# Two ends of a graph-and-attention layer: where the row work of two batches stands in the queues

## The chip, the cores and the metric

The kernel runs on one core of one Trainium2 chip. The time is the device time of one execution in microseconds, and a kernel's time is the median of its runs. The core has a matrix engine (TensorE, PE in the profile; PEld is its weight load), a vector engine (VectorE, DVE), an activation engine (ScalarE, ACT), a general engine (GpSimd, POOL) and a sync engine (SyncE, SP) whose queue issues every transfer of this kernel. Each engine takes its own instructions in the order in which they were written and waits on semaphores for those of others.

## The reference, cut to what matters

All numbers are float32. There are 16 batches of 1024 rows by 256 columns, and one 1024 by 1024 adjacency matrix. Two layers follow one another, each with a residual and a layer norm:

```python
# layer 0
agg = einsum('nm,bmd->bnd', A_hat, features)          # A_hat: the adjacency, normalised
h   = relu(_batchnorm(agg @ W1.T + b1, g1, be1))
out = _batchnorm(h @ W2.T + b2, g2, be2)              # statistics over all 16 batches
x   = _layernorm(x + out)
# layer 1, for each batch
c_adj = mean(x, axis=-1)                              # one mean per row
A     = abs(abs(sigmoid(c_adj[m] - c_adj[n]) - 0.5) - 0.5) * 2
Wg    = adj * (A + A.T) / 2                           # the gated adjacency
q     = relu((x.T @ Wg) * para)                       # the queries, by channel
k, v  = split(x @ kv_w)
out   = softmax(q k^T * scale) v                      # 4 heads of 64
x     = _layernorm(x + out)
```

The second batch norm of layer 0 needs its statistics over all batches, so layer 1 can't begin before layer 0 has ended.

## The kernel before

Layer 0 runs first and leaves its result, still without the second batch norm, in HBM (`yT`, as 128 by 128 blocks); the first batch's is fetched into SBUF before layer 0 ends. Layer 1 is the function `fast`. It goes batch by batch through 16 attention steps of each batch: two halves of 512 queries (`hf`), two pairs of heads (`pair`), four pairs of 128 keys (`cp`). A step writes scores to PSUM (`scores`, L783), takes exponentials on ScalarE (`exps`, L795), adds them up on VectorE for the denominators (`sums`, L801 and L804) and multiplies them with the values (`attend`, L819). TensorE is given the scores of step k+1 before the weighted sum of step k. After the last step of a pair the result is copied to SBUF (L830, L831) and, for all but the last half of the last batch, written to HBM.

Around the steps stands the work for the batches before and after. For the batch that comes two later: its rows are fetched (`load`: `yT` at L443, the residual at L447), scaled and shifted by the batch norm on GpSimd (`bn2_q`, L610), transposed and added on VectorE (`rows`, L614 and L615), given their statistics (`ln1_a`, with GpSimd's small operations at L66, L68 and L632) and normed on ScalarE (`ln1_b`, L642, which also sums each row). For the next batch: transposed rows (`x1_t` on TensorE, L671, for the first two batches), row means and the row of all means (`means` L675 and L677, `crow` L688 for batch 0; for the others one transpose at L692, a copy at L694, and a round trip through HBM at L695 and L696 that spreads it over the partitions), the gates (`wg_a` on ScalarE, L706 to L709; `wg_b` on VectorE, L715 and L716, after which the next block of the adjacency is loaded into the freed tile, L417), keys and values (L732, L743), and the products with the gated adjacency that give the queries (`graph`, L757; `queries`, L765 and L766). For the batch that has ended: the denominators (`dens`, L846 and L848), their reciprocals (`recips`, L857 and L859), and for each pair of row blocks `fetch_o` (L872), `finish_a` (transpose, division, residual and statistics: L888 to L901) and `finish_b` (norm on ScalarE, L909, and store, L912). In the last half of the last batch the result doesn't go through HBM: `finish_a` transposes it on TensorE (L885).

The order is written out by the program itself. `put(w, t, f, ...)` notes a piece for slot t of batch w; a slot is two steps, and a batch has eight. The last loop takes two slots at a time: `arrange` orders their pieces (those for TensorE spread among the long ones), all of them are issued, and then four attention steps. Pieces thus stand only ahead of every fourth step. `range_so_far` and `range_all` check that the denominators lie in a safe range; the flag of `range_all` is read at the end.

Batch 0 has nothing before it, so its row work, the keys, the values and the first three gates are issued outright ahead of the loop, with GpSimd's and ScalarE's work for it alone. Its queries come from `graph0` (L1074), which holds all four products in PSUM and goes through the eight row blocks one by one; they run in the slots of batch -1, one block in each (`opening`), with the remaining gates. Batch 1's row work stands in the same slots, by `put(b - 2, ...)`: `load` of row pair j in slot j, and what follows in the slots after it. `load` uses two buffers for the rows of `yT` and two for the residual; the adjacency has four.

Of the kernel before, what the change touches and what calls it, by code (L numbers as in the profile page):

```python
# [9 lines left out]
F32 = mybir.dt.float32  # L10
# [12 lines left out]
def gnn_norm_attention_kernel(  # L23
# [543 lines left out]
    def fast():  # L567
      with ExitStack() as fx:
# [48 lines left out]
        def begin(b):  # L617
            x1Ts[b] = x1Tp.tile([P, CT, N], F32, tag="x1T", name=f"x1T_{b}")
            css[b] = sm.tile([P, NT], F32, tag="cs", bufs=2, name=f"cs_{b}")
# [188 lines left out]
        def by_pe(b, hf):  # L808
            return b == B - 1 and hf == NH - 1
# [52 lines left out]

        OB = {}

        def fetch_o(b, j):
            hf, k = divmod(2 * j, KB)
            if by_pe(b, hf):
                return
            t = OB[b, j] = otp.tile([P, 2, C], F32, tag="ob", bufs=2, name=f"ob{b}_{j}")
            blk = o_dram[b, hf].rearrange("i (d e) (q n) -> q e (i d) n", e=Q, q=NQ)  # L870
            for q in range(NQ):
                nc.sync.dma_start(  # L872
                    t[q * Q : (q + 1) * Q].rearrange("p a (d n) -> p (a d) n", n=Q),
                    blk[q][:, ts(k // 2, 2 * C // Q), :],
                )

        def finish_a(b, j):
            hf, k = divmod(2 * j, KB)
            pool_r = (rp, "r") if b < B - 1 else (x1p, "x1")
            r = pool_r[0].tile([P, 2, C], F32, tag=pool_r[1], name=f"r_{b}_{j}")  # L880
            if by_pe(b, hf):
                p = ps_t.tile([P, 2, C], F32, tag="t", name="pf")
                for a in range(2):
                    for pair in range(NP):
                        nc.tensor.transpose(p[:, a, ts(pair, P)], OT[b, hf, pair][:, ts(k + a, P)], ident)  # L885
            else:
                p = r
                nc.vector.transpose(  # L888
                    r.rearrange("p a c -> p (a c)"), OB.pop((b, j)).rearrange("p a c -> p (a c)")
                )  # L890
            rd = RD[:, b * NT + 2 * j : b * NT + 2 * j + 2, :].rearrange("p a h -> p (a h)")
            nc.vector.tensor_mul(
                r.rearrange("p a (h d) -> p (a h) d", h=HEADS),
                p.rearrange("p a (h d) -> p (a h) d", h=HEADS),
                rd.unsqueeze(2).to_broadcast([P, 2 * HEADS, HD]),
            )
            nc.vector.tensor_add(r, r, x1s.pop((b, j)))
            mv, rs = ln_stats(sm, r, f"z{b}_{j}")
            nm = sm.tile([P, 2], F32, tag="nm", name=f"nm_{b}_{j}")
            for a in range(2):  # L900
                nc.gpsimd.tensor_scalar(  # L901
                    nm[:, a : a + 1], mv[:, a, 0:1], rs[:, a : a + 1], -1.0, op0=OP.mult, op1=OP.mult
                )
            R[b, j] = (r, rs, nm)
# [37 lines left out]

        NS = NT // 2 * NP * NH
        NC = NS // 2
        at = {}

        def put(w, t, f, *a):
            at.setdefault(w * NC + t, []).append((f, a))
# [4 lines left out]
        for b in range(B):  # L953

            for hf in range(NH):
                t = (hf + 1) * (NC // NH)
                put(b, t, dens, b, hf)
                put(b, t, recips, b, hf)
                for k in range(KB // 2):
                    j = hf * (KB // 2) + k  # L960

                    t_a, t_b = (t + 2 + k, t + 6 + k) if hf == 0 else (t + 4 + k, t + 6 + k)
                    if b == B - 1:
                        t_a, t_b = (t + 2 + k, t + 3 + k) if hf == 0 else (t + 1 + k, t + 2 + k)
                    put(b, t + 1, fetch_o, b, j)
                    put(b, t_a, finish_a, b, j)
                    put(b, t_b, finish_b, b, j)
            if b == 0:
                continue

            put(b - 2, 2, begin, b)
            for j in range(NT // 2):
                put(b - 2, j, load, b, j)
                put(b - 2, j + 1, bn2_q, b, j)
                put(b - 2, j + 2, rows, b, j)
                put(b - 2, j + 2, ln1_a, b, j)
                put(b - 2, j + 3, ln1_b, b, j)
                if b == 1:
                    put(b - 2, j + 4, x1_t, b, j)
                    continue  # L980
                put(b - 2, j + 3, put_x1, b, j)
                put(b - 2, 5 + j // 2 * 2, get_x1, b, j)
                put(b - 2, min(6 + j, NC), x1_v, b, j)
            put(b - 2, NC - 2, means, b)
            put(b - 2, NC - 1, crow, b)

            i = 0
            for t, n in enumerate(WG):
# [12 lines left out]
                    put(b - 1, NC - len(QG) + t, graph, b, m)  # L1001
                m += 1
        put(B - 1, 4, range_so_far)
        put(B - 1, NC + 1, range_all)

        nsteps = B * NS


        order = (dens, recips, x1_t, finish_a, fetch_o, finish_b, x1_v, rows, ln1_a, ln1_b, put_x1, get_x1, means, load, crow)
        rank = {f: k for k, f in enumerate(order)}  # L1010
        short = (dens, recips, x1_t)

        def is_short(fa):
            f, a = fa
            return f in short or f is finish_a and by_pe(a[0], 2 * a[1] // KB)

        long = (keys, values, graph)

# [9 lines left out]
        def arrange(pieces):  # L1028
# [1 line left out]
            gates = [fa for fa in pieces if fa[0] is gate]  # L1030
            many = [fa for fa in pieces if fa[0] in long]
            first += [fa for fa in pieces if fa[0] is bn2_q]
            alone = [fa for fa in pieces if fa[0] in (dens, recips, crow)]
            few = [fa for fa in pieces if fa not in first + gates + many + alone]
            few.sort(key=lambda fa: rank.get(fa[0], len(rank)))
            few_pe = [fa for fa in few if is_short(fa)]
# [15 lines left out]
                order = spread(order, gates)  # L1052


            for f, k in ((dens, 1), (recips, 2)):
                k = ([n for n, fa in enumerate(order) if fa[0] in long] + [len(order)] * 3)[k]
                order[k:k] = [fa for fa in alone if fa[0] is f]
            return first + order + [fa for fa in alone if fa[0] is crow]


# [8 lines left out]
        def graph0(k):  # L1069
# [11 lines left out]
            if k == NT - 1:  # L1081
                for h in range(NH):
                    for c in range(CT):
                        queries(0, c, h, PG0[h][:, c, :])

        begin(0)
        constants_q()
        for j in range(NT // 2):
            bn2(0, j)
        for j in range(NT // 2):  # L1090
            ln1_a(0, j)
        for j in range(NT // 2):
            ln1_b(0, j)
        x1_t(0, 0)
        x1_t(0, 1)
        keys(0, 0, 0)
        x1_t(0, 2)
        x1_t(0, 3)
        means(0)
        crow(0)  # L1100
        gate0(0)
        keys(0, 1, 0)
        for c in range(CT):
            keys(0, c, 1)
        gate0(1)
        values(0, 0)
        values(0, 2)
        gate0(2)
        values(0, 4)
        values(0, 6)  # L1110

        def opening(s):

            k = s + NC
            if 0 <= k < NC:
                for i in range(3 + 2 * k, min(5 + 2 * k, NT)):
                    gate0(i)
                graph0(k)

        NK = NT // 2
        for t in range(min(at) // 2, max(max(at) // 2, nsteps // NK - 1) + 1):
            g = NK * t
            now = [p for s in (2 * t, 2 * t + 1) for p in [(opening, (s,))] + arrange(at.get(s, []))]
            behind = max((k + 1 for k, fa in enumerate(now) if is_short(fa)), default=0)
# [6 lines left out]
            for k in range(g, g + NK):  # L1133
                if 0 <= k + 1 < nsteps:
                    scores(k + 1)
                    exps(k + 1)
                if 0 <= k < nsteps:
                    if k > g:
                        sums(k)
                    attend(k)  # L1140

        return nc.values_load(
            badi[0][0:1, 0:1],
# [163 lines left out]
```

## Time and profile before

The median of ten runs is 2493.79 us (2492.46 to 2495.62).

| what | value |
|---|---|
| the profiled execution's own time | 2491.68 us |
| its span, first to last instruction | 2489.9 us |
| TensorE busy | 2426.3 us, 97% |
| VectorE busy | 1794.7 us, 72% |
| ScalarE busy | 1096.0 us, 44% |
| GpSimd busy | 762.5 us, 31% |
| mean granted TensorE clock | 0.993 |

The profile is of one execution. A line of its timeline has the start, the duration, the engine, the line of the kernel, the operation, output and inputs, their sizes and a count; in brackets stands how long the engine was idle before it and what ended that. A float32 matmul leaves two records. Idle time of an engine that isn't the bound costs nothing.

### The profile page before, as it was taken

How to read it: one execution, taken by the hardware profiler on the slowest of the kernel's cores; microseconds unless marked ns; L12 is line 12 of the kernel's file. 1: busy time of each engine (PE TensorE's matmuls, PEld its weight loads, DVE VectorE, ACT ScalarE, POOL GpSimd, SP SyncE). 2: the span in 40 equal slices, each digit the busy share in tenths (PEclk: the TensorE clock that was granted, in tenths of full speed). 3: DMA queues.
4: the chain of work that ended last, by engine and by line, in shares of the span. 5: the costliest groups of instructions: out<-in, count | busy, mean ns of one | idle time of the engine just before them, and what ended most of it. 6: DMA issues, size and time to landing. Idle time of an engine off the chain costs nothing. (4 is left out here: it accounts for less than half of the span.)

```text
span 2489.9 us, 33864 instructions
## 1 busy us (share of the span) xinstructions
PE 2426.3 (97%) x12341; PEld 1018.4 (41%) x12341; DVE 1794.7 (72%) x2552; ACT 1096.0 (44%) x1549; POOL 762.5 (31%) x826
## 2 busy tenths in 40 slices
PE   8999999999999799999999999999999999999996
PEld 4444444443444443443434434344344343443432
DVE  5545555555777577888788888888888878887666
ACT  2000000003543455564655656656556465564554
POOL 2222222321656331313223133232341432423002
PEclk9999999999999899999999999999999999999998
DMA  3122222212676443544544535445354455453211
GB/s 135 68 85 102 86 83 85 101 72 80 245 278 229 119 119 84 133 120 110 140 114 109 141 83 147 112 119 145 89 137 112 113 138 114 110 143 87 72 39 40
DMA packets 563118, 288.66 MB, mean 116 GB/s; under 512 B 390664, under 2 KB 535680, under 8 KB 555776
## 3 DMA queue, kind: packets, MB, share of 16 engines
q1 hardware_dynamic: 562944, 286.43, 41.5%
q8 instruction: 99, 1.62, 0.3%
q14 instruction: 75, 0.61, 0.1%
HBM read 192.43 MB, written 93.91 MB: 115 GB/s over the span
## 5 line engine op out<-in xcount | busy, mean ns | idle before, releaser
L795 ACT ACTIVATE e<-s 128x1024 f32<-128x1024 f32 x512 | 496.3, 1021 | 339.3 <-PE s L783 287.4
L804 DVE TENSOR_TENSOR acc<-acc,e 128x1024 f32<-128x1024 f32 x384 | 506.7, 1319 | 121.6 <-ACT e L795 95.3
L783 PE MATMUL s<-qT,kT 64*64 64x512 f32 x4096 | 492.5, 596 | 13.1 <-ACT e L795 9.8
L819 PE MATMUL o<-e,v 64*64 64x512 f32 x4096 | 485.7, 589 | 0.0
L757 PE MATMUL pg<-wg,x 128*128 128x512 f32 x960 | 428.9, 597 | 0.0
L610 POOL TENSOR_TENSOR yt<-yt,stq 128x512 f32<-128x512 f32 x120 | 175.4, 1462 | 429.2 <-DMA yt<-yT 374.4
L783 PEld LDWEIGHTS s<-qT,kT 64*64 64x64 f32 x4096 | 147.3, 133 | 307.0 <-issue 261.0
L819 PEld LDWEIGHTS o<-e,v 64*64 64x64 f32 x4096 | 156.7, 133 | 283.9 <-issue 275.3
L757 PEld LDWEIGHTS pg<-wg,x 128*128 128x128 f32 x960 | 177.5, 190 | 231.4 <-issue 227.6
L103 ACT COPY u<-pa 128x512 f32<-128x512 f32 x15 | 8.8, 586 | 475.3 <-PE pa L308 475.3
L716 DVE SCALAR_TENSOR_TENSOR wg<-wg,adj 128x1024 f32<-128x1024 f32 x128 | 162.9, 1302 | 4.0 <-ACT wg L709 1.2
L66 POOL TENSOR_SCALAR rs_z<-mv_z 128x2 f32<-128x2 f32 x64 | 17.0, 265 | 478.3 <-DVE mv_z L559 396.7
L308 PE MATMUL pa<-AhT,x 128*128 128x512 f32 x360 | 161.8, 592 | 0.0
L831 DVE TENSOR_TENSOR ot<-o,ot 128x512 f32<-128x512 f32 x64 | 44.3, 692 | 153.0 <-ACT ot L830 153.0
L642 ACT ACTIVATE x<-x,nm_a,rs_a 128x256 f32<-128x256 f32 x128 | 75.9, 594 | 175.8 <-POOL nm_a L632 175.4
L732 PE MATMUL pk<-x1T,kvw 128*128 128x512 f32 x256 | 122.2, 612 | 1.3 <-DVE x1T L672 1.3
L66 POOL TENSOR_SCALAR rs_a<-mv_a 128x2 f32<-128x2 f32 x64 | 38.8, 606 | 257.4 <-DVE mv_a L559 236.4
L743 PE MATMUL pv<-kvw,x1T 128*128 128x256 f32 x512 | 117.1, 382 | 0.0
L339 PE MATMUL ph<-agg,SW 128*128 128x512 f32 x240 | 112.8, 592 | 0.0
L743 PEld LDWEIGHTS pv<-kvw,x1T 128*128 128x128 f32 x512 | 96.0, 190 | 31.5 <-issue 16.2
L308 PE MATMUL pa<-T,sx 128*128 128x512 f32 x240 | 107.9, 592 | 0.0
L308 PEld LDWEIGHTS pa<-AhT,x 128*128 128x128 f32 x360 | 68.4, 190 | 86.1 <-issue 86.1
(192 smaller groups left out, 3157.2 us busy)
## 6 DMA issues: line engine op xcount, KB each, us to landing
adj<-in_adj_dram SPq DMA_DIRECT2D x128, 512.0 KB, 4.4
h<-hT SPq DMA_DIRECT2D x28, 1024.0 KB, 4.4
hL<-h SPq DMA_DIRECT2D x28, 1024.0 KB, 9.1
x<-in_x_dram SPq DMA_DIRECT2D x16, 1024.0 KB, 7.2
yT<-y SPq DMA_DIRECT2D x64, 256.0 KB, 2.5
out_dram<-r SPq DMA_DIRECT2D x64, 256.0 KB, 2.3
xr<-in_x_dram SPq DMA_DIRECT2D x62, 256.0 KB, 3.4
o<-ot SPq DMA_DIRECT2D x62, 256.0 KB, 2.3
```

Source lines behind the costliest of these rows:

```text
L308: nc.tensor.matmul(p, xs[n][:, k, :], bs[n][:, k, :], start=(k == 0), stop=(k == KN - 1))
L339: nc.tensor.matmul(p, ws[n][:, ts(f, P)], bs[n], start=True, stop=True)
L610: nc.gpsimd.tensor_tensor(y, y, sc, op)
L642: nc.scalar.activation(r, r, AF.Identity, bias=nm[:, a : a + 1], scale=rs[:, a : a + 1], accum_out=css[b][:, i : i + 1])
L716: nc.vector.scalar_tensor_tensor(t, t, 1.0, adjs[b * NT + i], op0=OP.add, op1=OP.mult)
L732: nc.tensor.matmul(p, kvw[:, k, ts(c, P)], x1Ts[b][:, k, ts(h, FB)], start=(k == 0), stop=(k == CT - 1))
L743: nc.tensor.matmul(p[:, ts(a, C)], x1Ts[b][:, k, ts(j + a, P)], kvw[:, k, C:], start=(k == 0), stop=(k == CT - 1),)
L757: nc.tensor.matmul(pg[b], x1s[b, k // 2][:, k % 2, ts(c, P)], wgs[b, k][:, ts(h, FB)], start=(k == 0), stop=(k == NT - 1))
L783: nc.tensor.matmul(t[r * HD : (r + 1) * HD, h, :], kTs[b, pair][h * HD : (h + 1) * HD, ts(2 * cb + r, HD)], qTs[b, pair, hf][h * HD : (h + ...
L795: nc.scalar.activation(E[g, a], S.pop((g, a)), AF.Exp)
L804: nc.vector.tensor_add(ACC[b, hf, pair], ACC[b, hf, pair], E[g, a])
L819: nc.tensor.matmul(O[b, hf, pair][r][h * HD : (h + 1) * HD, :], vs[b][r * HD : (r + 1) * HD, cb, pair * P + h * HD : pair * P + (h + 1) * HD],
```

## The change

Both ends of layer 1 are ordered anew; no instruction is added or removed, except that the eight transposes of the last half come in two groups.

At the end, `finish_a` of the last half no longer holds its own transposes: `back` does them, issued together with the denominators and ahead of the reciprocals. For the last three halves (batch 14's second, batch 15's two) the pieces get other slots. A half that goes through HBM has its first `finish_a` in the middle of the four steps, behind the third one's sums (`between`), its second one slot pair later, and each `finish_b` two slots after its `finish_a`, but the second of batch 15's first half only behind the last step. `range_all` comes one slot later, behind the last rows.

At the opening, batch 1's row work is taken out of the slots and written out. Its first two loads stand right behind the first transposes of batch 0; its first two row pairs are scaled behind batch 0's last transposes and worked on behind gates 1 and 2; the rest follows `second_rows`, one entry behind each row block of `graph0`. `means(1)` and `crow(1)` come after the last block, behind batch 0's queries. Of batch 0's own pieces, the first norm and transpose move ahead of the last pair's statistics, the first values ahead of the first keys, and the means ahead of the third transpose.

```diff
+        def back(b, j):
+            hf, k = divmod(2 * j, KB)
+            p = OB[b, j] = ps_t.tile([P, 2, C], F32, tag="t", name="pf")
+            for a in range(2):
+                for pair in range(NP):
+                    nc.tensor.transpose(p[:, a, ts(pair, P)], OT[b, hf, pair][:, ts(k + a, P)], ident)
...
             if by_pe(b, hf):
-                p = ps_t.tile([P, 2, C], F32, tag="t", name="pf")
-                for a in range(2):
-                    for pair in range(NP):
-                        nc.tensor.transpose(p[:, a, ts(pair, P)], OT[b, hf, pair][:, ts(k + a, P)], ident)
+                p = OB.pop((b, j))
...
-                    t_a, t_b = (t + 2 + k, t + 6 + k) if hf == 0 else (t + 4 + k, t + 6 + k)
-                    if b == B - 1:
-                        t_a, t_b = (t + 2 + k, t + 3 + k) if hf == 0 else (t + 1 + k, t + 2 + k)
-                    put(b, t + 1, fetch_o, b, j)
-                    put(b, t_a, finish_a, b, j)
+                    if b * NH + hf < B * NH - 3:
+                        t_f, t_a, t_b = (t + 1, t + 2 + k, t + 6 + k) if hf == 0 else (t + 1, t + 4 + k, t + 6 + k)
+                    elif not by_pe(b, hf):
+
+                        t_f, t_a, t_b = t, t + 2 * k, t + 2 + 2 * k if b < B - 1 else (t + 2, NC + 1)[k]
+                    else:
+                        t_f, t_a, t_b = t, t + 1 + k, t + 2 + k
+                    put(b, t_f, back if by_pe(b, hf) else fetch_o, b, j)
+                    if t_a == t:
+                        between[(b * NC + t) * 2 + NK // 2] = [(finish_a, (b, j))]
+                    else:
+                        put(b, t_a, finish_a, b, j)
                     put(b, t_b, finish_b, b, j)
...
-        put(B - 1, NC + 1, range_all)
+        put(B - 1, NC + 2, range_all)
...
-        for j in range(NT // 2):
+        for j in range(NT // 2 - 1):
             ln1_a(0, j)
-        for j in range(NT // 2):
+        ln1_b(0, 0)
+        x1_t(0, 0)
+        ln1_a(0, NT // 2 - 1)
+        load(1, 0)
+        load(1, 1)
+        for j in range(1, NT // 2):
             ln1_b(0, j)
-        x1_t(0, 0)
         x1_t(0, 1)
+        values(0, 0)
         keys(0, 0, 0)
+        means(0)
         x1_t(0, 2)
         x1_t(0, 3)
-        means(0)
+        bn2_q(1, 0)
+        bn2_q(1, 1)
         crow(0)
         gate0(0)
         keys(0, 1, 0)
         for c in range(CT):
             keys(0, c, 1)
         gate0(1)
-        values(0, 0)
+        rows(1, 0)
+        ln1_a(1, 0)
+        load(1, 2)
         values(0, 2)
         gate0(2)
         values(0, 4)
         values(0, 6)
+        rows(1, 1)
+        ln1_a(1, 1)
+        load(1, 3)
+        begin(1)
+
+        second_rows = {
+            0: [(bn2_q, 2)],
+            1: [(bn2_q, 3)],
+            2: [(ln1_b, 0)],
+            3: [(rows, 2), (ln1_a, 2), (ln1_b, 1)],
+            4: [(x1_t, 0), (rows, 3), (ln1_a, 3)],
+            5: [(ln1_b, 2), (x1_t, 1)],
+            6: [(ln1_b, 3), (x1_t, 2)],
+            7: [(x1_t, 3)],
+        }
...
                 graph0(k)
+                for f, j in second_rows[k]:
+                    f(1, j)
+                if k == NC - 1:
+                    means(1)
+                    crow(1)
...
             for k in range(g, g + NK):
...
                     attend(k)
+                for f, a in between.pop(k, ()):
+                    f(*a)
```

## The prediction

> **What bounds the kernel now.** I read the page first, then TensorE's idle time in equal slices, then the timeline of every engine around the two slices that are not full, and last the waits of SP's queue.
>
> ```profile
> PE 2426.3 (97%) x12341; PEld 1018.4 (41%) x12341; DVE 1794.7 (72%) x2552; ACT 1096.0 (44%) x1549; POOL 762.5 (31%) x826
> PE   8999999999999799999999999999999999999996
> ```
>
> TensorE is the bound: 63.6 us of the 2489.9 us span are not matmul. The fourteenth slice (809 to 871 us, the opening of layer 1) and the last one hold most of it. The page's chain of waits stops at the last instruction, so it is of no use here. The same stretches in windows (columns: stretch, length, then busy time of PE, PEld, DVE, ACT and POOL, granted clock, DMA):
>
> ```profile
> 831.20:860.60 29.40, 29.38 (x86) 15.77 (x84) 17.40 (x22) 14.85 (x17) 2.10 (x2) 1.00 0.55 159
> 860.60:879.10 18.50, 13.59 (x38) 6.56 (x39) 10.52 (x25) 5.11 (x16) 12.38 (x22) 0.91 0.37 90
> 879.10:897.60 18.50, 15.17 (x82) 6.33 (x80) 13.85 (x18) 13.12 (x17) 3.12 (x3) 1.00 0.54 139
> 2454.40:2466.00 11.60, 3.77 (x24) 1.30 (x24) 10.06 (x18) 4.05 (x5) 5.46 (x7) 0.73 0.14 46
> ```
>
> So the opening loses 4.9 + 3.3 us and the tail 7.8 us, each with time at a lower clock behind it. The timeline says why (start, duration, engine, line, and in brackets the idle time ahead and what ended it):
>
> ```profile
> 835.28 14.01 SPq L417 DMA_DIRECT2D adj<-in_adj_dram  x5
> 849.40 1.96 SPq L443 DMA_DIRECT2D yt<-yT  x4
> 854.77 2.18 POOL L610 TENSOR_TENSOR yt<-yt,stq 128x512 f32<-128x512 f32 x2 [29.92 <-DMA yt<-yT]
> 865.44 1.27 PE L671 MATMUL px<-ident,x 128*128 128x128 f32 x4 [4.86 <-ACT x L642]
> 866.51 4.89 PE L1074 MATMUL pg<-wg,x 128*128 128x512 f32 x8
> 886.76 1.15 ACT L706 ACTIVATE wg<-crow,hcs 128x1024 f32<-128x1024 f32 x1 [2.44 <-DMA crow<-crow_d]
> 897.58 2.00 PE L783 MATMUL s<-qT,kT 64*64 64x512 f32 x16 [1.97 <-ACT e L795]
> ```
>
> In the opening, batch 1's rows are fetched at 849.40 because five adjacency loads stand ahead of them in SP's queue, each waiting for a gate to free its tile. Its transposes then stop TensorE for 4.86 us. At the end:
>
> ```profile
> 2445.42 7.87 DVE L804 TENSOR_TENSOR acc<-acc,e 128x1024 f32<-128x1024 f32 x6
> 2454.94 0.70 DVE L888 STREAM_TRANSPOSE r<-ob 128x512 f32<-128x512 f32 x1
> 2459.98 1.33 ACT L909 ACTIVATE r<-r,nm,rs_z 128x256 f32<-128x256 f32 x2 [6.38 <-POOL nm L901]
> 2462.27 3.69 PE L783 MATMUL s<-qT,kT 64*64 64x512 f32 x16 [7.83 <-ACT e L795]
> ```
>
> ScalarE stands at batch 15's first norm, which VectorE reaches late behind its sums; the exponentials are queued behind that norm, and TensorE behind them.
>
> **What the Trainium skill says.** "Perfetto Trace Analysis", Tensor Engine Instruction: ACT, DVE and GpSimd queues are strict first in, first out; the 6.38 us above, with scores already in PSUM, agree. "DMA: Bandwidth & Descriptors", Anatomy of one DMA: a DMA's semaphore wait is spent on the issuing sequencer; SP's 14.01 us for five loads agree. "TensorE: Matmul & The Clock Gate", What's actually happening: after an idle window of about 3.4 us the array runs at half rate for about as long; here 16 score records take 3.69 us after the stall and 1.90 us elsewhere. "SBUF — State Buffer", SBUF: two separate sides: a VectorE operation with two SBUF inputs and a GpSimd one lock each other out for a whole instruction; here GpSimd's four small operations for a norm take 1.6 us alone (2483.41 to 2485.03) and 5.0 us under VectorE's sums (2445.67 to 2450.68).
>
> **Opening, part by part.** No instruction is added or removed; they move.
> - Loads of batch 1's first two row pairs go ahead of all adjacency loads. SP is free after the constants at 823.75; four issues and the landing took 5.4 us before (849.40 to 854.77), so they land near 829 and 833. GpSimd's scaling (2.2 us each) and VectorE's rows (2.6 us each: transpose, add, statistics) now lie between the gates. Gates still come first where it counts: two rows put 5.3 us on VectorE, which had 2.6 + 1.5 us of waits between those gates, and each gate is needed only one 3.43 us group of products after the last. I cost this at nothing, hidden by the graph products; without cover it would be up to 5 us. Adjacency loads 5 to 7 are issued between 840 and 850 behind row loads, and take 3.6 us; their gates are due on TensorE at 859 or later.
> - So the 4.86 us stall goes, and with it the cold stretch: transposes from 865.44 to 866.51 instead of 0.44 us (0.63), eight product records in 4.72 us instead of 3.43 (1.29): 6.8 us.
> - One value group (8 of 32 records of 7.07 us) moves ahead of the keys, into the waits at 820 to 824: 1.77 us less on the path, minus some 0.15 us because the means now follow one key copy later: 1.6 us. The bounds are -0.5 and +3 us, the latter if TensorE, busier there, leaves the half rate before 828.
> - The means and the row of means of batch 1 now follow the queries. Let T be the last transposes (878.98). Before, the row's transpose ran at T + 0.43. Now VectorE first does eight query operations (4.24 us, 878.22 to 882.46), which start 1.5 us before T as the first product tile is complete, then the last copy (0.6) and two tiny scalings (0.2): T + 3.6. That is 3.15 us later, and in TensorE's queue the first scores stand behind it. Their two tiles then run without the 1.03 us wait between them. The keys follow near T + 6 to T + 7.5, depending on the clock; but ScalarE's gates wait for the row from HBM (landing 7.4 us after its transpose, as now), and the exponentials behind them set the next scores: 18.6 us after T now, 21.75 us then. The whole 3.15 us are lost.
> - Sum: 6.8 + 1.6 - 3.15 = 5.3 us gained. From there attention is bound by TensorE as before.
>
> **Tail, part by part.**
> - Row work of batch 14's second half and batch 15's first half is taken up two to four steps earlier on VectorE, between two steps' sums. The stall of 7.83 us goes, and its cold stretch: scores to sums 3.47 instead of 1.72 us, then 2.11 instead of 1.72: 2.1 us. Together 9.9 us.
> - ScalarE now has three pairs of norms instead of two ahead of one step's exponentials (1.04 us more, and perhaps 0.5 us of GpSimd's lock); the two pairs of before cost TensorE 0.4 us (at 2424.17), so nearly all of the added time shows: -1.5 us. A pair also stands ahead of the copy of the denominators (0.59 us, TensorE waits 0.71 us for it): -0.45 us.
> - Batch 15's first norm: on this kernel's clock VectorE would end its statistics near 2448.8 (exponentials of the step before end at 2443.57, sums 1.3 us a half, row work 3.43 us), GpSimd at 2450.4 alone or 2453.8 under sums, and ScalarE arrives at 2451.5. TensorE has about 1 us of slack there, so 0 to 1.6 us are lost; I take 0.9.
> - The eight last transposes now run together ahead of the reciprocals. From the end of the last weighted sum (A) the last norm ended 12.75 us later (2473.17 to 2485.92). Now: VectorE's six sums run to A + 1.4 (they queue behind the second row work), last output tile +0.7, transposes 1.2, denominators' transpose 0.7, reciprocal 0.3, two row works 2.7 each, and 2.67 from statistics to the last norm: 12.4. Gain 0.4 us. The range check now comes last on VectorE; its 1.4 us are covered by GpSimd and ScalarE's 2.67 us.
> - Output stores change places in SP's queue, but none stands ahead of a store that is ready earlier: nothing.
> - Sum: 9.9 - 1.5 - 0.45 - 0.9 + 0.4 = 7.45 us gained.
>
> **Total.** 12.75 us. The profiled execution took 2491.68 us, 2.1 us under the median of the ten runs (2493.79); 2491.68 - 12.75 = 2478.9 and, at the median, 2481.0.
>
> **Rivals.**
> 1. The opening gives nothing: the early rows and gates get in each other's way on VectorE (up to 5 us), or the late row of means costs more than 3.15 us. For it: VectorE is the engine that takes all the moved work. Against: several microseconds of slack at every gate. Then only the tail counts: 2486.
> 2. The tail's wait moves rather than goes: GpSimd takes 5.0 us under the sums at both early norms and VectorE is a sum or two later than I worked out, so ScalarE waits 3 to 4 us there. For it: the 5.0 us are in this trace. Against: a full step's room now. Tail 4, total 9: 2485.
> 3. Slower: batch 1's first rows come so late that VectorE, in order, holds the gates of tiles 2 and up behind them. They now depend on the constants' round trip through HBM (7.4 us in the waits of SP) and two loads. Rows reach VectorE near 840, the scaled tile is ready near 832, and the gate has another 4 us: it decides from a landing 12 us late. To end 5 us above the present time it would have to be 30 us late; the slowest kind of load on the page takes 9.1 us to land.
> 4. No change within measurement: gains of both ends fall to under 5 us together.
>
> **How the numbers follow.** Forecast (9 to 17 us gained) 0.68; rival 1 0.12; rival 2 0.11; rival 4 0.05; rival 3 or another loss 0.04. The likeliest one's own range is 2476.5 to 2485; the bounds of the unknown costs (opening 3 to 8 us, tail 5 to 10) and rivals 1 and 2 take it to 2475.5 to 2488. About 0.2% (5 us) is what a measurement of this kernel can tell from no change: faster 0.90, same 0.06, slower 0.04.
>
> **What would show it.** In the changed profile: yt loads near 824, no wait ahead of batch 1's first transposes, product groups without a gap from about 841.6 to 870; a gap of about 3 us ahead of the row's transpose near 874; the second step's scores near 892.5. In the tail no wait over 2 us at the exponentials, and the last norm about 12 us after the last weighted sum. I am wrong if TensorE waits at a gate, if the wait at batch 15's first norm is still over 3 us, or if new gaps appear between the two ends.

## The result, and the profile after

The changed kernel takes 2476.33 us (median of 8 runs, 2474.98 to 2479.11); the kernel before, measured again beside it and with its ten first runs, 2493.79 us (28 runs). The ratio is 0.9931, 95% interval 0.9922 to 0.9939: 17.5 us or 0.7% faster. The forecast was 2481.0 us, 12.75 us faster, with a range of 2475.5 to 2488. The direction held. The range held too, but only by 0.8 us: the gain is 4.7 us larger than forecast, and it lies above the 9 to 17 us that the prediction gave for its own forecast. The profiled execution after has a span of 2472.9 us, 17.0 us under the span before.

The engines' busy times on the page after, and TensorE's in 40 equal slices:

```profile
PE 2423.7 (98%) x12341; PEld 1019.3 (41%) x12341; DVE 1796.0 (73%) x2552; ACT 1095.5 (44%) x1549; POOL 778.8 (31%) x826
PE   8999999999999899999999999999999999999997
```

Now 49.2 us of the span are not matmul, where it was 63.6: 14.4 of the 17.0 us are idle time of TensorE. The other 2.6 us are busy time (2426.3 to 2423.7 us for the same matmuls, of which fewer run at half rate, that is at a granted clock of 0.50). The slice that showed 7 at the opening shows 8. The windows of the same stretches, after (stretch, length, busy time of PE, PEld, DVE, ACT, POOL, granted clock, DMA):

```profile
829.40:856.90 27.50, 27.50 (x78) 14.40 (x77) 22.27 (x35) 16.67 (x24) 20.25 (x18) 1.00 0.76 210
856.90:868.50 11.60, 11.60 (x37) 5.73 (x36) 5.95 (x12) 2.55 (x8) 2.47 (x7) 1.00 0.00 0
868.50:888.90 20.40, 16.88 (x78) 6.97 (x76) 13.80 (x18) 13.02 (x17) 3.98 (x3) 0.92 0.51 133
2443.80:2455.40 11.60, 11.60 (x113) 3.97 (x104) 10.31 (x15) 7.37 (x9) 5.94 (x7) 1.00 0.08 25
```

From the second group of keys to batch 1's last transposes TensorE is never idle, though VectorE works for 22.27 us and GpSimd for 20.25 us of the first 27.5 us. The tail's stretch is full too. What is left is the third line: 3.5 us idle and a clock of 0.92 around the row of means. The timeline of the opening, after:

```profile
822.89 2.95 PE L743 MATMUL pv<-kvw,x1T 128*128 128x256 f32 x8
823.66 3.29 SPq L443 DMA_DIRECT2D yt<-yT  x4
825.68 1.88 PE L732 MATMUL pk<-x1T,kvw 128*128 128x512 f32 x4
829.44 2.18 POOL L610 TENSOR_TENSOR yt<-yt,stq 128x512 f32<-128x512 f32 x2 [3.64 <-DMA yt<-yT]
839.74 17.33 PE L1082 MATMUL pg<-wg,x 128*128 128x512 f32 x40
856.91 0.60 PE L671 MATMUL px<-ident,x 128*128 128x128 f32 x4
868.52 0.60 PE L671 MATMUL px<-ident,x 128*128 128x128 f32 x4
872.16 0.27 PE L692 MATMUL pc<-ident,cs 128*8 128x128 f32 x1 [3.04 <-DVE cs L675]
872.61 3.55 PE L783 MATMUL s<-qT,kT 64*64 64x512 f32 x16 [0.18 <-issue]
878.15 1.15 ACT L706 ACTIVATE wg<-crow,hcs 128x1024 f32<-128x1024 f32 x1 [0.91 <-DMA crow<-crow_d]
888.96 2.01 PE L783 MATMUL s<-qT,kT 64*64 64x512 f32 x16 [0.37 <-ACT e L795]
```

The rows of batch 1 are fetched 26 us earlier (823.66 instead of 849.40), and its first transposes (856.91) have no wait in brackets where 4.86 us stood. The products start at 839.74, not 843.25; that is twice as much as forecast, and the line of the keys says why: four records in 1.88 us where the kernel before needed 3.78:

```profile
824.37 3.78 PE L732 MATMUL pk<-x1T,kvw 128*128 128x512 f32 x4 [1.27 <-DVE x1T L672]
```

The last transposes come at 868.52 instead of 878.98. Then the 3.04 us of the late row of means, as forecast, with first scores at half rate after it (3.55 us for 16 records, elsewhere 1.90). The second step's scores stand at 888.96, 8.62 us earlier than before. The tail:

```profile
2412.53 3.06 ACT L911 ACTIVATE r<-r,nm,rs_z 128x256 f32<-128x256 f32 x6
2416.54 2.00 PE L783 MATMUL s<-qT,kT 64*64 64x512 f32 x16 [1.10 <-ACT e L795]
2429.26 0.66 PE L857 MATMUL pr<-ident,dt 128*128 128x128 f32 x4 [1.14 <-ACT dt L848]
2444.50 0.50 POOL L903 TENSOR_SCALAR nm<-mv_z,rs_z 128x1 f32<-128x1 f32 x2
2444.80 1.09 ACT L911 ACTIVATE r<-r,nm,rs_z 128x256 f32<-128x256 f32 x2 [0.38 <-POOL nm L903]
2447.06 1.90 PE L783 MATMUL s<-qT,kT 64*64 64x512 f32 x16
2467.16 1.09 ACT L911 ACTIVATE r<-r,nm,rs_z 128x256 f32<-128x256 f32 x2 [1.48 <-POOL nm L903]
```

The three pairs of norms ahead of one step (first two lines) cost TensorE a wait of 1.10 us; the pair ahead of the denominators' copy raises the wait of 0.71 us to 1.14. At batch 15's first norm ScalarE waits 0.38 us where it waited 6.38, and the scores behind it start without a wait. The last weighted sum ends at 2455.82, the last norm at 2468.25: 12.43 us, forecast 12.4.

Where the gain lies can be read off one kind of line that comes once in each half of a batch, the matmuls of the denominators (L846). The thirtieth and the last of these lines, in the kernel before and then in the changed one:

```profile
2404.30 1.07 PE L846 MATMUL pd<-acc,ones 128*32 128x512 f32 x8
2473.10 1.06 PE L846 MATMUL pd<-acc,ones 128*32 128x512 f32 x8
```

```profile
2395.69 1.06 PE L846 MATMUL pd<-acc,ones 128*32 128x512 f32 x8
2455.75 1.05 PE L846 MATMUL pd<-acc,ones 128*32 128x512 f32 x4
```

From the first (937.01 before) to the thirtieth (2404.30 before) all of them stand 8.60 to 8.62 us earlier after the change: the middle 1500 us are moved as a block, and nothing is gained or lost there. At the thirty-first (2434.68 before) it is 7.63, at the last 17.35, at the end of the last norm 17.67. So the opening gave 8.6 us and the tail 9.06 us up to the last norm, and 0.67 us were lost behind it (4.65 us from the last norm to the end of the span, before 3.98).

### The profile page after: what moved, and what is told of

It is laid out like the page before. It is cut to its first block, busy times and chain, and to the rows that moved or that the text cites. A ratio compares the mean times of both kernels' runs of the same rounds, so it can differ in the third digit from the quotient of the medians.

```text
span 2472.9 us, 33867 instructions
## 1 busy us (share of the span) xinstructions
PE 2423.7 (98%) x12341; PEld 1019.3 (41%) x12341; DVE 1796.0 (73%) x2552; ACT 1095.5 (44%) x1549; POOL 778.8 (31%) x826
## 3 DMA queue, kind: packets, MB, share of 16 engines
q8 instruction: 99, 1.62, 0.3%
## 5 line engine op out<-in xcount | busy, mean ns | idle before, releaser
L610 POOL TENSOR_TENSOR yt<-yt,stq 128x512 f32<-128x512 f32 x120 | 183.4, 1529 | 403.0 <-DMA yt<-yT 295.8
```

The lines of the kernel that those rows point to most:

```text
L610: nc.gpsimd.tensor_tensor(y, y, sc, op)
```

## The experiments

In each kernel below, the lines of the denominators again tell the tail from the rest. The opening is measured from the first transposes of batch 0 (814.42 before, 814.43 after), since what layer 0 takes varies between executions: in one profile below it came 2.9 us later, with the same instructions. From there to the second step's scores it is 83.16 us before and 74.53 after. Times are medians beside runs of the kernel before on the same chip, which took 2492.9 to 2493.75 us. The changed kernel was not run again beside them, so a difference from its 2476.33 us carries the 0.9 us by which the kernel before moved, and the intervals are some 3.5 us to each side. Where parts of a few us are told apart, it is by the profiles, of one execution each.

### The opening alone, and the tail alone

The kernel before with the opening's part of the diff, and the changed kernel with the opening of the kernel before.

> The kernel before with the new opening alone; the ends of batches 14 and 15 as before. Nothing is left out. Theory (the two ends are independent, and the opening gave more than forecast): the second step's scores stand near 889.0 us as in the changed kernel, not at 897.6, and the kernel is 8.6 us faster than before (ratio 0.9965); the stall of 7.8 us at batch 15's first norm is still there. Rival (the forecast's own sum was right and the rest of the gain came from the tail): 5.3 us faster (ratio 0.9979). Second rival (part of the opening's gain was a lucky landing of the row of means, 6.0 us after its transpose instead of 7.4): 7.3 us faster or less, and the landing again near 7.4 us.

> The changed kernel with the old opening: only the ends of batches 14 and 15 are changed. Nothing is left out. Theory: the tail gives 9.0 us (ratio 0.9964): the stall of 7.83 us and its cold stretch of 2.1 us go, the three pairs of norms ahead of one step's exponentials cost 1.0 us, the pair ahead of the copy of the denominators 0.4 us, and batch 15's first norm costs nothing. Rival (the forecast on record): 7.45 us (ratio 0.9970), with 0.9 us lost at batch 15's first norm. Second rival (the two parts help each other, for example because the stream of batch work reaches the tail in another phase): less than 7 us here.

Opening alone: 2485.02 us, ratio 0.9963 (0.9949 to 0.9977), 8.7 us faster. Tail alone: 2484.12 us, ratio 0.9958 (0.9944 to 0.9971), 9.6 us faster. Together 18.3 us, both at once 17.5: within these intervals the parts are independent, and each gave more than forecast (5.3 and 7.45). By the profile the tail alone gives 9.07 us from the thirtieth denominators to the last norm; with the new opening it was 9.06. These two agree to a hundredth.

The opening doesn't repeat so well, and this is the first of three things hidden in its 8.6 us. Around the row of means, the timeline of the opening alone, and then of the tail alone (with the old opening):

```profile
872.23 0.27 PE L692 MATMUL pc<-ident,cs 128*8 128x128 f32 x1 [3.04 <-DVE cs L675]
879.18 1.15 ACT L706 ACTIVATE wg<-crow,hcs 128x1024 f32<-128x1024 f32 x1 [1.84 <-DMA crow<-crow_d]
890.00 2.01 PE L783 MATMUL s<-qT,kT 64*64 64x512 f32 x16 [1.30 <-ACT e L795]
```

```profile
867.00 1.27 PE L671 MATMUL px<-ident,x 128*128 128x128 f32 x4 [6.57 <-ACT x L642]
881.78 0.27 PE L692 MATMUL pc<-ident,cs 128*8 128x128 f32 x1
887.33 1.15 ACT L706 ACTIVATE wg<-crow,hcs 128x1024 f32<-128x1024 f32 x1 [0.65 <-DMA crow<-crow_d]
898.15 2.00 PE L783 MATMUL s<-qT,kT 64*64 64x512 f32 x16 [0.18 <-ACT e L795]
```

In the first the gate that needs the row starts 6.95 us after the row's transpose; in the changed kernel, with the same order of instructions there, it was 5.99. In the second it is 5.55 us, where the kernel before had 7.35, and a stall of 6.57 us, where it had 4.86. So the row's trip through HBM (5.55 to 7.35 us over all these profiles) and the old stall scatter by almost 2 us from one execution to the next. Over the executions with the new opening unaltered (this one, the changed kernel, and four below) the opening takes 74.2 to 75.5 us, 74.9 in the mean, and over the two with the old one 83.2 and 83.9: the gain of 8.6 us is also the difference of the means, but its parts in a single pair of profiles are partly luck. In the profile of the opening alone, where the row landed late, the gain is 7.64 us (83.16 less 75.52), close to the second rival's bound of 7.3. So that rival is right on the landing, and wrong on the sum only in the mean, in which the old opening has two profiles.

### The first value group back in its old place

```diff
         x1_t(0, 1)
-        values(0, 0)
         keys(0, 0, 0)
...
         load(1, 2)
+        values(0, 0)
         values(0, 2)
```

> The changed kernel with the first value group back behind the second gate, where it was. Nothing is left out. Theory A (the group does two things: its 1.77 us fill a wait, and TensorE, kept busy at 820 to 824 us, leaves its half rate some 2 us earlier): the first keys take 3.8 us instead of 1.9 again, the graph products start near 843.2 instead of 839.7, and the kernel is 3.5 us slower than the changed one (ratio to before 0.9945). Theory B (only the 1.77 us move, and the clock would have come up anyway because the other moves of the opening keep TensorE busy): 1.6 to 1.8 us slower (ratio 0.9938), and the first keys take 1.9 us.

2478.96 us, ratio 0.9939 (0.9925 to 0.9953), 2.6 us slower than the changed kernel by the medians, whose intervals are too wide to choose between 1.7 and 3.5. The profile chooses:

```profile
822.16 1.15 PE L671 MATMUL px<-ident,x 128*128 128x128 f32 x4
824.93 3.78 PE L732 MATMUL pk<-x1T,kvw 128*128 128x512 f32 x4 [1.62 <-DVE x1T L672]
828.51 1.13 PE L671 MATMUL px<-ident,x 128*128 128x128 f32 x8
843.45 2.74 PE L1082 MATMUL pg<-wg,x 128*128 128x512 f32 x6
```

The keys take 3.78 us again, and the products start 28.80 us after the first transposes instead of 25.31: 3.49 us. Theory A holds, and this is the second thing hidden in the opening's 8.6 us. The group fills a wait with 1.6 us of its own work, and the keys behind it no longer run at half rate: 1.90 us more.

The record of the granted clock shows how. In all twelve profiles here the clock changes only at steps of 3.41 us or a multiple of it. With the value group first, TensorE works without a gap from 820.03 on, and the full clock is granted from 825.02, ahead of the keys. With the group back, TensorE stands for 1.62 us ahead of the keys, and the full clock comes at 828.70, behind them. The Trainium skill fits: "TensorE: Matmul & The Clock Gate", What's actually happening, has the array leave the half rate after about 3.4 us of work, and by time, not by the number of matmuls. The transposes count as work here. In the kernel before they stood alone ahead of 821, and the full clock was there and went again, as TensorE waited for 1.60 and 0.78 us between them (stretches of before):

```profile
818.00:821.00 3.00, 1.25 (x8) 0.58 (x7) 2.83 (x9) 1.28 (x4) 2.48 (x7) 1.00 0.00 0
821.50:824.50 3.00, 1.41 (x5) 0.72 (x5) 2.71 (x7) 2.12 (x8) 2.46 (x7) 0.50 0.00 0
```

So the group pays twice because it closes a gap in TensorE's work. The keys took 1.88 us in all nine profiles with the group first and 3.78 us in the three with it behind, wherever the steps of the clock lay.

### The row of means ahead of the queries

```diff
-            6: [(ln1_b, 3), (x1_t, 2)],
-            7: [(x1_t, 3)],
+            6: [(ln1_b, 3), (x1_t, 2), (x1_t, 3)],
+            7: [],
...
+                if k == NC - 1:
+                    means(1)
                 graph0(k)
...
                 if k == NC - 1:
-                    means(1)
                     crow(1)
+                    for h in range(NH):
+                        for c in range(CT):
+                            queries(0, c, h, PG0[h][:, c, :])
```

(and `graph0` no longer issues the queries itself)

> The changed kernel with the last transposes of batch 1 ahead of the last group of products, the means of batch 1 ahead of that group on VectorE, and the row of means ahead of the queries. Nothing is left out. With T the end group of products: the row's transpose runs at once after it instead of 3.04 us late. Theory A (the late row of means costs what it is late, as the prediction has it): the first scores start at once and warm (1.9 us instead of 3.55), the second step's scores come 1.9 to 3.2 us earlier than in the changed kernel (885.7 to 887.1 us instead of 888.96), and the kernel is faster than the changed one by as much: ratio to before 0.9918 to 0.9923 instead of 0.9931. Theory B (the row's landing is hidden behind keys, values and gates, and TensorE's own work sets the second step's scores): TensorE's wait moves behind the first scores, and the gain is under 0.5 us.

2472.9 us, ratio 0.9916 (0.9902 to 0.9929), 3.4 us faster than the changed kernel; 3.2 by the profile:

```profile
869.00 0.27 PE L692 MATMUL pc<-ident,cs 128*8 128x128 f32 x1
869.29 1.09 PE L783 MATMUL s<-qT,kT 64*64 64x512 f32 x8
871.41 1.09 PE L783 MATMUL s<-qT,kT 64*64 64x512 f32 x8 [1.03 <-DVE qT L765]
874.96 1.15 ACT L706 ACTIVATE wg<-crow,hcs 128x1024 f32<-128x1024 f32 x1 [1.37 <-DVE acc L801]
885.77 2.00 PE L783 MATMUL s<-qT,kT 64*64 64x512 f32 x16 [0.89 <-ACT e L795]
```

The row's transpose comes 3.16 us earlier, its gate 5.96 us after it, as good as equal to the 5.99 of the changed kernel, and the second step's scores 3.19 us earlier: theory A, and one to one. (The bracket of the gate names VectorE's sum, which ended 0.11 us before it. The gate doesn't need that sum: in the changed kernel it starts at 878.15, and the sum ends at 878.49.) This settles the third thing. In the forecast the late row cost its whole 3.15 us; the two profiles of before and after seem to say 1.84 (18.60 us from the last transposes to the second step's scores before, 20.44 after). But the trip of the row took 7.35 us in the one and 5.99 in the other. Taken out: before 18.60 - 7.35 = 11.25, after 20.44 - 5.99 = 14.45, the opening alone 21.41 - 6.95 = 14.46, with the value group back 21.65 - 7.20 = 14.45. The late row costs 3.2 us, and the forecast had it right. (In the two profiles of the new opening with the shortest trips, 5.57 and 5.67 us, the scores wait for nothing, 20.2 us after the last transposes.)

### The loads late

```diff
-        load(1, 0)
-        load(1, 1)
...
-        bn2_q(1, 0)
-        bn2_q(1, 1)
...
         gate0(1)
+        load(1, 0)
+        load(1, 1)
+        bn2_q(1, 0)
+        bn2_q(1, 1)
         rows(1, 0)
```

> The changed kernel with the first two loads of batch 1's rows back behind the first two adjacency loads in SP's queue (they then wait for the gates that free those tiles), and the two scalings on GpSimd behind the second gate; VectorE's order is as in the changed kernel, the rows ahead of the third gate. Nothing is left out. The loads are issued near 838 us instead of 823.7 and land near 843.5 instead of 829.4, some 14 us late. The prediction's third rival held that VectorE has slack for a landing 12 us late, so by it 2 us are lost against the changed kernel. By the changed kernel's trace the rows then end on VectorE near 848.6, the third gate near 850.7, and TensorE wants it at 846.6: a wait of 4 us ahead of the third group of products, 1 to 1.5 us more at the fourth, and a half-rate stretch after it[...]: 5 to 7 us slower than the changed kernel, that is no faster than 2481 us. If the early loads don't matter at all, no wait at the gates and no loss.

2481.98 us, ratio 0.9952 (0.9937 to 0.9967), 5.7 us slower than the changed kernel.

```profile
843.47 2.18 POOL L610 TENSOR_TENSOR yt<-yt,stq 128x512 f32<-128x512 f32 x2 [17.41 <-DMA yt<-yT]
845.68 0.71 DVE L614 STREAM_TRANSPOSE x<-yt 128x512 f32<-128x512 f32 x1 [7.98 <-DMA yt<-yT]
849.35 1.23 DVE L716 SCALAR_TENSOR_TENSOR wg<-wg,adj 128x1024 f32<-128x1024 f32 x1
850.63 13.35 PE L1082 MATMUL pg<-wg,x 128*128 128x512 f32 x24 [3.48 <-DVE wg L716]
```

The rows land 14.0 us later than in the changed kernel, VectorE stands 7.98 us at them with the third gate behind, and TensorE waits 3.48 us for that gate and then works 24 records in 13.35 us where 10.4 would do (17.33 for 40). The rows between the gates are free only because the loads are early. The slack was 10.5 us (14.0 less the wait of 3.5), not the 12 of the third rival, and what is late beyond it costs nearly double: 3.5 us of wait and 3.0 of half rate behind it. The rival's mechanism is real, but it took a transfer two adjacency loads further back to call it up; no wait came at the fourth gate, where 1 to 1.5 us were expected.

### Which half's row work counts in the tail

The slots of one half put back to those of the kernel before, the other left early: first batch 14's, then batch 15's.

```diff
-                    if b * NH + hf < B * NH - 3:
+                    if b * NH + hf < B * NH - 2:
```

```diff
+                    elif (b, hf) == (B - 1, 0):
+                        t_f, t_a, t_b = t + 1, t + 2 + k, t + 3 + k
                     elif not by_pe(b, hf):
```

> The changed kernel in which the row work and norms of batch 14's second half stand where they stood before, and only those of batch 15's first half are early. Nothing is left out. Theory A (VectorE must be cleared of batch 14's 6.9 us of row work first; moving batch 15's alone only puts it behind that): ScalarE waits some 5 us at batch 15's first norm, TensorE stands about as long, a half-rate stretch follows, and the kernel is 4 to 7 us slower than the changed one (ratio to before 0.995 to 0.996). Theory B (early issue of batch 15's first half is what counts): no TensorE wait over 2 us, and within 1.5 us of the changed kernel.

> The changed kernel in which the row work and norms of batch 15's first half stand where they stood before, and only those of batch 14's second half are early: the counterpart of moving batch 15's alone, which kept a wait of 6.91 us. Nothing is left out. Theory A (both moves are needed: batch 15's first norm needs 3.4 us of row work and 2 to 5 us of GpSimd after VectorE reaches it, and in its old place it is reached only in the step whose exponentials stand behind the norm): ScalarE waits 5 to 7 us there, TensorE about as long, and the kernel is 5 to 9 us slower than the changed one. Theory B (a VectorE clear of batch 14 is enough): a wait under 3 us, at most 3 us slower.

Batch 15's alone early: 2481.14 us, ratio 0.9953 (0.9938 to 0.9968). Batch 14's alone: 2483.66 us, ratio 0.9962 (0.9951 to 0.9974). That is 4.8 and 7.3 us slower than the changed kernel. One line from each:

```profile
2452.29 3.69 PE L783 MATMUL s<-qT,kT 64*64 64x512 f32 x16 [6.91 <-ACT e L795]
```

```profile
2454.52 3.69 PE L783 MATMUL s<-qT,kT 64*64 64x512 f32 x16 [6.28 <-ACT e L795]
```

From the thirtieth to the last denominators the two together gain 8.74 us, batch 15's alone 1.09, batch 14's alone 0.40. A part of the loss comes back at the end. Where TensorE stands, VectorE catches up: with batch 15's alone its last sums end 0.55 us ahead of the end of the last weighted sum, in the changed kernel 1.59 us behind it. The last norm then ends 11.11 us after the last weighted sum in both kernels, instead of 12.43. Up to the last norm the gains are 9.06, 2.7 and 2.0 us. Theory A holds in both: with batch 14's two row works of 3.43 us still ahead, VectorE reaches batch 15's first rows late (statistics end at 2444.9, 3.5 us later than in the changed kernel); with them gone but batch 15's in the old slot, it reaches them only in the step whose exponentials already stand behind the norm. Neither is a half of the gain: the wait is there as long as either cause is.

### The norms one to a step, and both edits together

```diff
-                    put(b, t_b, finish_b, b, j)
+                    if b == B - 2:
+                        between.setdefault(b * NS + (17, 18, 21, 25)[j], []).append((finish_b, (b, j)))
+                    else:
+                        put(b, t_b, finish_b, b, j)
```

> The changed kernel with the four last pairs of norms of batch 14 one at a time: each is issued on ScalarE behind the exponentials of a step of its own, instead of three pairs ahead of one step's exponentials and one ahead of the copy of the denominators. Nothing is left out. Theory A (those norms cost TensorE what ScalarE's 1.45 us of idle time in a step cannot hold: 0.98 us at the three pairs and 0.43 us at the copy, as read from where TensorE's denominators stand in the changed kernel and in the one before): both waits go, 1.4 us faster than the changed kernel (ratio to before near 0.9925). Theory B (the norms are no loss, because VectorE's row work or GpSimd's lock sets the steps there): the waits of TensorE stay, or come back at a step whose norm waits for GpSimd; within 0.4 us of the changed kernel.

> The changed kernel with both edits: the row of means ahead of the queries, and batch 14's four last pairs of norms one to a step. Nothing is left out. If both gains are on the path and apart from each other (1500 us lie between them), it is 3.2 + 1.4 = 4.6 us faster than the changed kernel: some 2471.5 us, ratio to before 0.9912. If the norms' gain isn't real, 2472.9 us as with the row of means alone.

The norms alone: 2475.6 us, ratio 0.9922 (0.9909 to 0.9936); 0.7 us under the changed kernel, which by the times alone is nothing. Its profiled execution is the one in which layer 0 took 2.9 us longer, so only positions count: from the thirtieth to the last denominators it gains 10.55 us on the kernel before, the changed kernel 8.74. That is 1.81 us, where 1.4 were expected, since the 0.4 us that two pairs cost already before go too. ScalarE's norms in that profile:

```profile
2406.42 1.94 ACT L795 ACTIVATE e<-s 128x1024 f32<-128x1024 f32 x2 [1.49 <-PE s L783]
2408.25 1.09 ACT L911 ACTIVATE r<-r,nm,rs_z 128x256 f32<-128x256 f32 x2
2409.91 1.94 ACT L795 ACTIVATE e<-s 128x1024 f32<-128x1024 f32 x2 [0.57 <-ACT r L911]
```

One pair fits into the 1.5 us that ScalarE idles in a step, with half a microsecond to spare. With the row of means ahead as well: 2470.55 us, ratio 0.9905 (0.989 to 0.9921), 5.8 us better than the changed kernel and 23.2 better than the one before. Expected was 2471.5. It is the fastest of all.

### The range check back

```diff
-        put(B - 1, NC + 2, range_all)
+        put(B - 1, NC + 1, range_all)
```

> The changed kernel with the range check back between the last two row works on VectorE, where it was; the eight last transposes stay together and early. Nothing is left out. The changed kernel ends 4.65 us after its last norm, the one before 3.98. Theory A (the late range check holds the end: the flag is read last): here the end comes 3.95 us after the last norm again, but VectorE's last row work starts 0.65 us later, so the last norm ends 13.1 us after the last weighted sum instead of 12.4, and the time is within 0.2 us of the changed kernel. Theory B (the end is set by the last stores, which now follow each other at 2.6 us instead of 4.1): the 4.65 us stay or shrink a little, and the kernel is 0.3 to 0.7 us slower than the changed one. Either way no more than 0.7 us, below what the runs can tell; the profile is read.

2477.15 us, ratio 0.9938 (0.9922 to 0.9955), not to be told from the changed kernel. By the profile the last norm ends 13.53 us after the last weighted sum instead of 12.43, and the end comes 4.32 us later instead of 4.65. Theory A falls: the 3.95 us did not come back. The check's place is worth 1.1 us of the end chain (0.65 expected). What follows the last norm goes with how far apart the two last norms are, and with them the last two stores: 4.1 to 4.5 us apart, 3.94 to 3.98 us to the end; 3.7 apart, 4.32; 2.6 apart, 4.5 to 4.9 in the nine other profiles with the new end. That the stores hold each other up is an inference from these numbers; nothing here measures it alone.

## Why the prediction was right, and low

Step by step, forecast against the profiles:

| step of the prediction | forecast, us | measured, us |
|---|---|---|
| stall and cold stretch at batch 1's transposes | +6.8 | +6.94 (last transposes 10.46 earlier, less 3.52 of the earlier products) |
| value group into the waits | +1.6 | +3.5 (3.49 when undone) |
| means and row of means behind the queries | -3.15 | -3.2 at equal trips of the row; -1.84 in this pair of profiles |
| stall and cold stretch of the tail | +9.9 | +10.15 (the 8.74 to the last denominators, with the 0.98 and 0.43 of the next rows added back) |
| third pair of norms ahead of one step | -1.5 | -0.98 |
| pair ahead of the denominators' copy | -0.45 | -0.43 |
| batch 15's first norm | -0.9 | 0 |
| end chain to the last norm | +0.4 | +0.32 |
| behind the last norm | none | -0.67 |
| sum | 12.75 | 17.0 |

**The mechanisms held, but for the value group and the stores.** Early loads end the stall, rows lie free between the gates, the late row of means costs all that it is late, the tail's stall goes because both halves' row work is taken up early, and the norms cost what ScalarE's idle time can't hold. No rival came true as a whole: the opening gave 8.6 us and not nothing, the tail's wait did not move (0.38 us on ScalarE, none on TensorE), and the loads land 10.5 us ahead of the point from which they hurt.

**The term that was mis-sized is the value group,** 1.9 of the missing 4.3 us. The prediction counted only the group's own 1.77 us. The other half stood in it as the bound of "+3, the latter if TensorE, busier there, leaves the half rate before 828"; it did so, at 825.02 by the record of the granted clock, and the 3.78 us of the four key records, which the trace before shows to be twice what they take elsewhere, could have been entered at half. Here work that was moved into a wait ahead of a half-rate stretch was paid twice.

**Another 1.3 us are the trip of the row,** 7.35 us in the profile before and 5.99 after. The forecast took the same trip for both, which is the right thing to do, and its 21.75 us from the last transposes to the second step's scores are met in the executions in which the trip was long (21.65 at 7.20). No forecast from one profile can have this term; it is a reason for a range. With equal trips the opening would have gained 7.3 us in this pair. That the difference of the means is 8.6 all the same rests on the old opening's second profile, where the trip was short (5.55 us) but the stall 1.7 us longer; with two profiles of the old opening, how much of the 1.3 us is luck stays open.

**At the norms I erred on the safe side,** by 0.5 and 0.9 us. Of GpSimd's small operations for batch 15's first norm two ran under VectorE's sums (1.03 and 1.74 us, where they take 0.22 and 0.71 alone), but the last pair ran clear of them (0.50 us, under sums 2.06), and the 0.38 us that ScalarE then waited lie within TensorE's slack of 1 us. The estimate had the right bounds, 0 to 1.6, and the value in their middle. Against this stand 0.67 us behind the last norm, which I had at nothing with the sentence that no store stands ahead of one that is ready earlier. The 12.4 us of the end chain were met, but their gain of 0.32 is two things: the two kernels that keep a wait at batch 15's first norm have 11.11 us, so 1.64 us came from the new order, and 1.32 went again because without the wait VectorE still has sums to do.

## What to carry to other kernels

A row of loads behind loads that wait for buffers is a dependency that no engine's timeline shows: read the issuing queue, and when the loads are moved forward, count how late they may land before in-order work behind them is held. Where a wait on one engine has two causes in a row, moving either alone can gain little (1.09 and 0.40 us here to the last denominators, 8.74 together), so such changes must be priced and tried as one. Small work for an engine with idle time in each step belongs one piece to a step, not ahead of every fourth: the same four pairs of norms cost 1.8 us in one place and nothing in the other.

## What the hardware showed that I had not expected

- Transposes brought the full clock as products did. In four of the twelve profiles (the kernel before, the tail alone, batch 15's alone, the norms alone) it was full for one step of 3.41 us with transposes alone ahead of it (817.89 to 821.30 before), and half again after it. In the other eight the transposes ahead of 820 did not bring it; the steps of the clock lie elsewhere there. The Trainium skill says that transposes don't count as busy in the same way ("TensorE: Matmul & The Clock Gate", Part 4: PE-mode transpose); these float32 transposes counted.
- A wait of 3.04 us already put the scores behind it at half rate (16 records in 3.15 to 3.64 us instead of 1.90 in the eight profiles that have it), for one step of 3.41 us (872.81 to 876.22 in the changed kernel). The 3.48 us at the third gate did the same for two steps. The Trainium skill has about 3.4 us for this ("TensorE: Matmul & The Clock Gate", What's actually happening), and says that the window runs free of the kernel; the wait here was shorter.
- A row of 4 KB that goes to HBM and comes back to all partitions is ready for ScalarE 5.55 to 7.35 us after its transpose, in executions that are alike in everything around it. What makes the difference was not tried.
